# A chained kernel of four layers: in the last one, a block's first products issued ahead of the preceding block's second products

## The chip, the cores and the metric

The program runs on one core of one Trainium2 chip, in one launch. The core has TensorE (PE in the profile, its weight loads shown apart as PEld), VectorE (DVE), ScalarE (ACT), GpSimd (POOL) and SyncE (SP), which only issues transfers here. Each engine works through its own queue of instructions in order; semaphores join them. The metric is the device time of the whole program in microseconds, as the median of the runs.

## The reference, cut to what matters

Four layers follow one another on x of shape (8, 64, 64, 64): a selective scan, a channel and spatial attention, a small network that is trained for two steps on its own input (layer 2), and a spatial attention (layer 3). The change lies where layer 2's trained network is applied and layer 3 begins:

```python
def _modifier(params, x):
    w1, gn_w, gn_b, w2 = params
    h = jnp.einsum('bchw,oc->bohw', x, w1)        # first products
    ...
    h = hg.reshape(b, o, hh, ww) * gn_w[None, :, None, None] + gn_b[None, :, None, None]
    h = _gelu(h)
    return jnp.einsum('bohw,co->bchw', h, w2)     # second products
...
modification = _modifier(params_f, x)
...
return x + residual_scale * gate * modification   # end of layer 2

# layer 3
xb = jnp.einsum('oc,ncl->nol', wb, xf) + bb[None, :, None]
xc = jnp.einsum('oc,ncl->nol', wc, xf) + bc[None, :, None]
xd = jnp.einsum('oc,ncl->nol', wd, xf) + bd[None, :, None]
attention = jnp.einsum('nci,ncj->nij', xc, xb)
att = jax.nn.softmax(attention, axis=-1)
x_o = jnp.einsum('ncj,nij->nci', xd, att).reshape(n, c, h, w)
return alpha[0] * x_o + x
```

## The kernel before, in words

The eight images are worked on in four pairs: the 64 channels of two images fill the 128 partitions, and the 64 x 64 = 4096 positions lie along the free dimension, in NBK = 8 blocks of BK = 512. Everything is float32.

The function `modifier_and_attention` first trains the network (`moments`, then two rounds of `prepare`, `slope`, `gradients`, `update`). In `slope` (L1767 to L1790) the network is applied as well: there the first products of each block are issued one block ahead of the second products, by the list `late`. Then, for each pair p (L2125), it

- loads x of the pair (L2126, `load_pair` at L1635), into one of two buffers;
- applies the trained network block by block (L2127 to L2132): `mod.hidden` makes the first products of both images (L1751, two products of 64 x 512 into the tile hnps) and their Gelu (L1753, two activations of 128 x 512 into the tile a); `mod.output` makes the second products (L1762, two products into the two halves of the tile yps); one VectorE instruction (L2130) adds the gated result to x in place;
- stores x (L2134) for the attention's general case, and a small matrix for each image (L2136);
- makes keys (kps, L1137) and values (vps, L1148) of the whole pair in `att.project`;
- runs the attention in `att.run`: for each block of 512 queries, the query product (qps, L1170) with its bias (L1172), then for 32 groups of 128 keys the scores (sc, L1179), their exponential (ex, L1184), the running sum (L1191) and the values' product (av, L1198). At the end of a block of queries `divide` (L1207 to L1222) sums, takes the reciprocal (L1213) and scales, and `finish` (L2138) adds x and stores the result.

```python
def hidden(self, p, x):
    ...
    ps = self.two()
    ...
    return a
def output(self, a):
    ps = self.bank("yps")
    ...
    return ps
```

The tiles hnps, yps, kps, vps and sc all come from one PSUM pool with three buffers of two banks each (`p_sc`, tag "sc", L2116, L2119, L2120), handed out in turn in the order of the source. The Gelu's tile a has two buffers (tag "h"), the query tile q two, and the query product and the sums of the division share one PSUM bank (`p_psum`, tag "mm", L2115).

The order of instructions on each engine in this part is set by a scheduler that starts from the order of the source and may move an instruction ahead where its inputs are there. In this kernel it has moved the query products of the first three blocks of queries, L1170, from the attention up into the loop of L2127: PE's order there is first products, a query product (in three of the blocks), second products of the same block, first products of the next.

Of the kernel before, what the change touches and what calls it, by code (L numbers as in the profile page):

```python
# [13 lines left out]
ALU = mybir.AluOpType  # L14
# [8 lines left out]
BK = 512  # L23
NBK = L // BK
# [2063 lines left out]
def modifier_and_attention(cm, x2, w, a, x3, mixes, out):  # L2088


    tc, nc = cm.tc, cm.nc
    with ExitStack() as ctx:
        cm.open(ctx, "m_const")
        keep = ctx.enter_context(tc.tile_pool(name="m_keep", bufs=1))
        with ExitStack() as train:
            work = train.enter_context(tc.tile_pool(name="t_work", bufs=2))
            psum = train.enter_context(tc.tile_pool(name="t_psum", bufs=2, space=PSUM))
            mod = Modifier(cm, keep, x2, w, work, psum)
            tok = train.enter_context(tc.tile_pool(name="t_tok", bufs=1))
            wide = train.enter_context(tc.tile_pool(name="t_wide", bufs=2, space=PSUM))  # L2100
            accs = train.enter_context(tc.tile_pool(name="t_acc", bufs=2, space=PSUM))
            mod.two = lambda: wide.tile([128, 2, BK], F32, name="hnps", tag="dps")
            ys = tok.tile([2 * C, NB // 2, L], F32, name="ys")
            mod.moments(tok.tile([128, NB, TQ, C], F32, name="xT"), ys)
            gs = mod.gates()
            for s in range(STEPS):
                mod.prepare(wide)
                mod.slope(ys)
                mod.gradients(ys, wide, accs)
                mod.update(s == 0)  # L2110
            mod.settle()
            mod.prepare(wide)
        work = ctx.enter_context(tc.tile_pool(name="m_work", bufs=2))
        mod.xp = ctx.enter_context(tc.tile_pool(name="m_x", bufs=2))
        psum = ctx.enter_context(tc.tile_pool(name="p_psum", bufs=1, space=PSUM))  # L2115
        sc = ctx.enter_context(tc.tile_pool(name="p_sc", bufs=3, space=PSUM))  # L2116
        avp = ctx.enter_context(tc.tile_pool(name="p_av", bufs=1, space=PSUM))
        mod.psum, mod.work = psum, work
        mod.bank = lambda name: sc.tile([128, 2, BK], F32, name=name, tag="sc")[:, 0, :]  # L2119
        mod.two = lambda: sc.tile([128, 2, BK], F32, name="hnps", tag="sc")  # L2120
        att = Attention(
            cm, ctx, "pa", C, a["wc"], a["bc"], a["wb"], a["bb"], a["wd"], a["bd"],
            a["alpha"], work, psum, sc, avp,
        )
        for p in range(NB // 2):  # L2125
            x = mod.load_pair(mod.xp.tile([2 * C, L], F32, name="x", tag="x"), p, slice(0, L))  # L2126
            for j in range(NBK):  # L2127
                blk = bass.ts(j, BK)
                y = mod.output(mod.hidden(p, x[:, blk]))
                nc.vector.scalar_tensor_tensor(  # L2130
                    x[:, blk], y, gs[:, p : p + 1], x[:, blk], ALU.mult, ALU.add
                )  # L2132

            nc.sync.dma_start(x3[2 * p : 2 * p + 2].rearrange("b c l -> (b c) l"), x)  # L2134
            for b in (2 * p, 2 * p + 1):
                nc.sync.dma_start(mixes[b], cm.ident[:C, :C])  # L2136

            def finish(i, o, p=p, x=x):  # L2138
                blk = bass.ts(i, BK)
                nc.vector.scalar_tensor_tensor(o, o, att.bv, x[:, blk], ALU.add, ALU.add)  # L2140
                nc.sync.dma_start(
                    out[2 * p : 2 * p + 2].rearrange("b c h w -> (b c) (h w)")[:, blk], o
                )

            k, v = att.project(p, x)
            att.run(p, x, k, v, finish)
        bad, src = att.out_of_range(), att.src
    with tc.If(bad > 0):
        general_attention(cm, src, x3, mixes, out.rearrange("b c h w -> b c (h w)"))


@with_exitstack
def conv_seq_kernel(ctx: ExitStack, tc: tile.TileContext, t: dict, out: bass.AP):
    def layer(i):
        p = f"L{i}_conv_"
        return {n[len(p) :]: v for n, v in t.items() if n.startswith(p)}

    dr = ctx.enter_context(tc.tile_pool(name="stream", bufs=1, space=DRAM))
    xh = dr.tile([NB, C, L], F32, name="xh")
    x1 = dr.tile([NB, C, L], F32, name="x1")  # L2160
    x2 = dr.tile([NB, C, L], F32, name="x2")
    x3 = dr.tile([NB, C, L], F32, name="x3")
    mix1 = dr.tile([NB, C, C], F32, name="mix1")
    mix3 = dr.tile([NB, C, C], F32, name="mix3")
    cm = Common(ctx, tc)
    scan_layer(cm, t["x"], layer(0), xh)
    gate_and_attention(cm, xh, layer(0), layer(1), x1, mix1, x2)
    modifier_and_attention(cm, x2, layer(2), layer(3), x3, mix3, out)
# [21 lines left out]
```

## Time and profile before

| | us |
|---|---|
| median of 3 runs | 12229.28 |
| lowest and highest | 12226.62, 12230.54 |
| the profiled execution: its own time | 12228.28 |
| the profiled execution: span of its instructions | 12226.5 |
| PE busy in the span | 11196.6 |
| DVE busy | 10380.4 |
| ACT busy | 7575.7 |
| first products of pair 0 begin | 10102.05 |
| keys begin, pairs 0, 1, 2, 3 | 10134.79, 10661.47, 11189.76, 11716.43 |
| first products begin, pairs 1, 2, 3 | 10631.21, 11157.88, 11686.17 |

The rows with a start are positions in the span, counted from its first instruction. A row of the timeline gives the start of a run of like instructions, how long the run took, the engine, the line of the kernel, the operation and its tiles (written tile first), and in brackets how long the engine had been idle before and which instruction ended that. A row of the stages gives, for a stretch of the span, the busy time of each engine with the number of instructions, then the clock that TensorE was granted (1.00 is full) and the transfers. A matmul's duration in a row overlaps with the next one's, so a distance is read from start to start. A float32 product of one block is two instructions in the profile.

### The profile page before, as it was taken

The numbers are of one execution on the slowest core, as the hardware profiler recorded it, in microseconds if no ns is written. First come the engines' busy times: TensorE is split into PE (matmuls) and PEld (weight loads), VectorE is DVE, ScalarE is ACT, GpSimd is POOL, SyncE is SP. The second block draws the span as 40 slices with busy tenths as digits, with TensorE's granted clock in tenths as the row PEclk, the third lists the DMA queues.
The fourth block names the chain that finished last, engine by engine and source line by source line (L and its number), as shares of the span: only waits on it lengthen the run. The fifth ranks groups of instructions, "written<-read, shape, count | busy, mean of one in ns | idle before, by whom it ended". The sixth has DMA issues, their size and how long they took to land. (4 is left out here: it accounts for less than half of the span.)

```text
span 12226.5 us, 120204 instructions
## 1 busy us (share of the span) xinstructions
PE 11196.6 (92%) x39087; PEld 4103.2 (34%) x39087; DVE 10380.4 (85%) x7400; ACT 7575.7 (62%) x10304; POOL 7247.3 (59%) x3326
## 2 busy tenths in 40 slices
PE   7899999999999999999998799999987779999999
PEld 2233333333333333333322233232335463333333
DVE  4999999999999999999999776868778676676767
ACT  4666667766667676676675554645547574555554
POOL 4999999999999999999999500000007480000000
PEclk8999999999999999999999899999998779999999
DMA  3666666666666666666666400000011100000000
GB/s 112 205 210 217 210 211 214 212 212 210 213 212 207 210 216 209 212 213 211 205 203 211 135 20 25 6 25 8 17 49 34 41 20 24 19 4 19 5 11 6
DMA packets 522899, 1528.62 MB, mean 125 GB/s; under 512 B 125312, under 2 KB 142352, under 8 KB 519696
## 3 DMA queue, kind: packets, MB, share of 16 engines
q1 hardware_dynamic: 522256, 1520.80, 37.9%
q8 instruction: 312, 5.11, 0.2%
q14 instruction: 331, 2.71, 0.1%
HBM read 1439.63 MB, written 72.09 MB: 124 GB/s over the span
## 5 line engine op out<-in xcount | busy, mean ns | idle before, releaser
L816 POOL TENSOR_TENSOR ct<-ct,h 128x1024 f32<-128x1024 f32 x2048 | 4789.4, 2362 | 296.8 <-DVE h L811 133.1
L882 PE MATMUL yps<-ct,lno_cen 128*128 128x512 f32 x8192 | 4119.9, 633 | 58.6 <-ACT yps L869 57.2
L811 DVE TENSOR_TENSOR_SCAN h<-a,state,z 128x1024 f32<-128x1024 f32 x1536 | 3570.4, 2341 | 82.5 <-ACT z L777 39.7
L762 ACT ACTIVATE a<-dt,amat 128x1024 f32<-128x1024 f32 x2048 | 2347.1, 1147 | 1134.8 <-DVE h L811 1128.1
L1191 DVE TENSOR_TENSOR sum<-sum,ex 128x1024 f32<-128x1024 f32 x1920 | 2347.5, 1223 | 618.5 <-ACT ex L1184 483.1
L1184 ACT ACTIVATE ex<-sc 128x1024 f32<-128x1024 f32 x2048 | 1968.0, 1024 | 1359.6 <-PE sc L1179 1359.2
L882 PEld LDWEIGHTS yps<-ct,lno_cen 128*128 128x128 f32 x8192 | 1476.4, 195 | 2078.9 <-issue 1818.0
L807 DVE TENSOR_TENSOR z<-z,e 128x1024 f32<-128x1024 f32 x1536 | 1859.8, 1211 | 128.0 <-PE z L780 75.5
L1198 PE MATMUL av<-ex,v 128*64 128x512 f32 x8192 | 1950.0, 604 | 0.0
L1179 PE MATMUL sc<-q,k 16*128 16x512 f32 (+1 forms) x8192 | 1562.1, 623 | 4.2 <-ACT q L1172 3.1
L780 PE MATMUL z<-bs,pick 48*128 48x512 bf16 x3072 | 941.9, 387 | 388.4 <-DVE h L811 339.5
L811 DVE TENSOR_TENSOR_SCAN h<-a,z 128x1024 f32<-128x1024 f32 x512 | 1161.3, 2281 | 75.0 <-ACT z L777 59.8
L770 POOL TENSOR_TENSOR bt<-bt,e 128x1024 f32<-128x1024 f32 x512 | 1209.8, 2363 | 5.4 <-DMA bt<-bc 5.4
L1505 POOL TENSOR_TENSOR gt<-gt,pad 128x1024 f32<-128x1024 f32 x16 | 34.9, 2179 | 1575.0 <-ACT gt L1504 1575.0
L1198 PEld LDWEIGHTS av<-ex,v 128*64 128x64 f32 x8192 | 512.2, 136 | 1332.7 <-issue 1278.9
L1179 PEld LDWEIGHTS sc<-q,k 16*128 16x128 f32 (+1 forms) x8192 | 528.2, 184 | 1016.4 <-issue 977.4
L777 ACT COPY z<-bt 128x1024 f32<-128x1024 f32 x512 | 519.9, 1015 | 406.0 <-DVE h L811 309.2
L780 PEld LDWEIGHTS <-pick 48*128 48x128 bf16 x3072 | 175.9, 95 | 1514.5 <-DVE h L811 931.4
L534 PE MATMUL vps<-pad,convd 128*128 128x512 f32 x1152 | 573.8, 599 | 0.1
L1878 DVE RECIPROCAL r<-e 128x512 f32<-128x512 f32 x128 | 420.6, 3322 | 0.0
L1881 POOL TENSOR_TENSOR r<-r,half 128x512 f32<-128x512 f32 x128 | 162.7, 1271 | 361.9 <-issue 186.0
L798 ACT COPY state<-h 128x1 f32<-128x1 f32 x2048 | 362.9, 177 | 0.0
(417 smaller groups left out, 9594.8 us busy)
## 6 DMA issues: line engine op xcount, KB each, us to landing
ct<-bc SPq DMA_DIRECT2D x2048, 512.0 KB
bt<-bc SPq DMA_DIRECT2D x512, 512.0 KB
x<-x SPq DMA_DIRECT2D x12, 2048.0 KB
bc<-e SPq DMA_DIRECT2D x128, 128.0 KB
x<-x SPq DMA_DIRECT2D x32, 512.0 KB
part<-x SPq DMA_DIRECT2D x128, 128.0 KB
bsd<-bp SPq DMA_DIRECT2D x192, 64.0 KB
bs<-bsd SPq DMA_DIRECT2D x128, 96.0 KB
```

What stands on the lines that cost most here:

```text
L534: nc.tensor.matmul(held[0].rearrange("p (r c) -> p r c", c=S), convd[:, t, :], pad[:, j * rows + dy : (j + 1) * rows + dy, dx : dx + S], s ...
L762: ctl["exp", n] = nc.scalar.activation(ctl["a", n], ctl["dt"], AF.Exp, scale=amat[:, ctl["k"], n : n + 1])
L770: nc.gpsimd.tensor_tensor(bt, bt, ctl["dus"], ALU.mult)
L780: nc.tensor.matmul(z[:, bass.ts(i, BK)], pick[:, n : n + 1].to_broadcast([3 * N, DI]), ctl["bs"][:, bass.ts(i, BK)], start=True, stop=True,)
L807: first = nc.vector.tensor_tensor(z, z, ctl["dus"], ALU.mult)
L811: nc.vector.tensor_tensor_scan(h[:, flip], a[:, flip], z[:, flip], 0.0 if state is None else state[:, n : n + 1], ALU.mult, ALU.add,)
L816: freed[at] = nc.gpsimd.tensor_tensor(ct, ct, h, ALU.mult)
L882: nc.tensor.matmul(ctl["ps"][:, bass.ts(i, BK)], lno_cen, ct[:, bass.ts(i, BK)], start=False, stop=(n == N - 1 and not ctl["turns"]),)
L1179: nc.tensor.matmul(sc[:, e, :], k[r : r + d, bass.ts(j, 128)], qs[i][r : r + d, :], start=True, stop=True,)
L1184: nc.scalar.activation(ex, sc, AF.Exp)
L1191: nc.vector.tensor_tensor(sums[i], sums[i], ex, ALU.add)
L1198: nc.tensor.matmul(avs[i][r, :], v[:, j, r], ex[:, e, :], start=(j == 0), stop=(j == TQ - 1))
```

## The change

In the loop over the blocks of a pair, the Gelu tiles go into a small table, the loop runs one turn longer, and each turn first issues the first products and Gelu of block j, and then the second products and the update of block j - 1. No computation is added or removed.

```diff
         for p in range(NB // 2):
             x = mod.load_pair(mod.xp.tile([2 * C, L], F32, name="x", tag="x"), p, slice(0, L))
-            for j in range(NBK):
-                blk = bass.ts(j, BK)
-                y = mod.output(mod.hidden(p, x[:, blk]))
-                nc.vector.scalar_tensor_tensor(
-                    x[:, blk], y, gs[:, p : p + 1], x[:, blk], ALU.mult, ALU.add
-                )
+            acts = {}
+            for j in range(NBK + 1):
+                if j < NBK:
+                    acts[j] = mod.hidden(p, x[:, bass.ts(j, BK)])
+                if j:
+                    blk = bass.ts(j - 1, BK)
+                    nc.vector.scalar_tensor_tensor(
+                        x[:, blk], mod.output(acts.pop(j - 1)), gs[:, p : p + 1], x[:, blk],
+                        ALU.mult, ALU.add,
+                    )
```

In the program that comes of it, PE's order in this part is: first products of blocks 0 and 1, then second products and first products in turn, the second products of blocks 6 and 7 one after the other, the keys, the values, and then the query product of the first block of queries. All eight query products of a pair stand behind the values: none is moved into the loop. ScalarE's order follows PE's, and the load of the exponential's table stands behind the first query's bias. The orders of VectorE, GpSimd and SyncE are the same as before.

## The prediction

> **What bounds the kernel now.** I read the chain of waits first, because the change can pay only where it runs.
>
> ```profile
> PE 19%; issue 3%; POOL 1%; DVE 1%; ACT 1%; DMA 0%; SPq 0%; ACTq 0%; DVEq 0%; POOLq 0%
> PE sc L1179 8%; PE av L1198 8%; PE htps L1847 1%; PE acc L1927 1%; PE yps L1762 1%; PE hnps L1751 0%; POOL t L1882 0%; POOL run L1916 0%; POOL t L1883 0%; POOL r L1881 0%; DMA x<-x 0%; ACT L1866 0%; ACT t L1866 0%; PE qps L1170 0%; PE vps L1148 0%
> ```
>
> The followed chain covers the last quarter of the span, and in the last layer it is TensorE (PE). Next the busy time by stage, for the modifier stage of pair 1 and for its attention stage (the columns are the stretch, its length, then PE, PEld, DVE, ACT and POOL busy, PEclk, DMA share, GB/s):
>
> ```profile
> 10630.00:10662.00 32.00, 25.60 (x78) 6.61 (x74) 11.51 (x15) 13.25 (x20) 0.00 (x0) 1.00 0.21 74
> 10700.00:11150.00 450.00, 450.00 (x1950) 150.31 (x1950) 321.74 (x281) 235.93 (x252) 0.00 (x0) 1.00 0.01 5
> ```
>
> In attention PE is never idle, so every microsecond put on or taken off PE there counts in full. In the modifier stage no engine is full: it is a relay. The timeline of pair 1 shows it (start, length, engine, line, operands; in brackets the idle time before and who ended it):
>
> ```profile
> 10631.21 1.13 PE L1751 MATMUL hnps<-x,hwp 64*128 64x512 f32 x4
> ...
> 10632.39 1.26 ACT L1753 ACTIVATE a<-hnps,off 128x512 f32<-128x512 f32 x2
> 10633.13 1.65 PE L1762 MATMUL yps<-a,w2T 128*64 128x512 f32 x4 [0.79 <-ACT a L1753]
> 10634.71 1.13 PE L1751 MATMUL hnps<-x,hwp 64*128 64x512 f32 x4
> ...
> 10637.26 0.74 DVE L2130 SCALAR_TENSOR_TENSOR x<-yps,gp,x 128x512 f32<-128x512 f32 x1
> 10638.06 1.13 PE L1170 MATMUL qps<-x,pa_wq 128*128 128x512 f32 x2 [2.22 <-DVE x L2130]
> ...
> 10650.79 1.13 PE L1751 MATMUL hnps<-x,hwp 64*128 64x512 f32 x4
> ...
> 10652.03 1.26 ACT L1753 ACTIVATE a<-hnps,off 128x512 f32<-128x512 f32 x2 [2.29 <-PE hnps L1751]
> 10652.77 1.65 PE L1762 MATMUL yps<-a,w2T 128*64 128x512 f32 x4 [0.85 <-ACT a L1753]
> 10654.35 1.13 PE L1751 MATMUL hnps<-x,hwp 64*128 64x512 f32 x4
> ```
>
> Call a block's first products h (L1751), its Gelu g (L1753), its second products y (L1762), its update u (L2130). From h to h one block takes 10654.35 - 10650.79 = 3.56 us: h, then PE waits for g, then y. Two things are lost per block: the 0.85 us wait, and y itself, which starts on the first half of g and stretches to 1.58 us (10654.35 - 10652.77) because the second half comes 0.6 us later. Three blocks of a pair also hold one query product (qps, L1170) between h and y; they take 3.56 us too, so those three ride free.
>
> **The change, step by step.** No instruction is added or removed except waits; h and g of block j+1 move ahead of y of block j. h and g issue no DMA, and nothing moves on SP or POOL; DVE's order stays.
>
> *The steady block.* The trace has the same two products in the new order already: the slope pass (L1787), which also issues h one block ahead.
>
> ```profile
> 9162.63 1.13 PE L1751 MATMUL hnps<-x,hwp 64*128 64x512 f32 x4
> ...
> 9163.69 1.08 PE L1762 MATMUL yps<-a,w2T 128*64 128x512 f32 x4
> ...
> 9164.70 1.13 PE L1751 MATMUL hnps<-x,hwp 64*128 64x512 f32 x4
> ...
> 9165.76 2.57 PE L1762 MATMUL yps<-a,w2T 128*64 128x512 f32 x8
> ```
>
> Start to start: h 1.06, y 1.01, so a block is 2.07 us with nothing between. The last row is a run of two y with no h between, 2.50 up to where the next could start: the second one again meets a Gelu half finished. Will g keep up here? It starts 1.24 us after its h (10652.03 - 10650.79) and ends at 2.50; the new order starts y 1.06 + 1.01 + 1.06 = 3.13 after that h. Spare 0.63.
>
> *New wait.* h, y and later kps share three PSUM buffers (tag "sc"). Given out in the order h0 h1 y0 h2 y1 h3 y2 ..., h(j+1) gets the buffer of y(j-2) and so waits for u(j-2). In the steady part u ends 0.1 + 0.75 us after its y, and h(j+1) comes 2.07 us after it: no stall. Behind h on PE stand all later products, so at a pair's start the wait does bite: u0 stands behind the previous pair's last division on DVE and ends at 10638.0 (row 10637.26 + 0.74). h3 cannot start before 10638.06, exactly where the query product waits today. PE has then done h0 h1 y0 h2 y1, against h0 y0 h1 before.
>
> *Pairs 1 and 3.* From 10638.06 there remain h3 to h7, y2 to y5, and the two last y: 5 x 1.06 + 4 x 1.01 + 2.50 = 11.84, so the keys (kps) start at 10649.90 instead of 10661.47: 11.57 saved; pair 3 has the same spacing. *Pair 2* spends 1.62 us more today (31.88 from first h to kps against 30.26), at a granted clock of 0.50 from 11165.9 to 11169.3. I weigh that below and take 11.57 again.
>
> *Pair 0* starts cold: PE waited for x until 10102.05, and the granted clock is 0.50 until 10111.0. y0 can start where it does now, 10106.53, and ends at 10109.0 as now, or near 10108.3 if the clock comes up one window (3.41 us) earlier because PE is denser. After it come 6 h, 5 y and the two last y, 13.91 us; h2 alone takes about 1 us more in the cold case. So kps starts near 10122.2 or 10123.9; today 10134.79. Saved 10.9 to 12.6; I take 11.7.
>
> Sum of the stages: 3 x 11.57 + 11.7 = 46.4 us.
>
> *What is given back.* The cover of the three query products goes with the relay. In the changed program they stand after the values product (vps) and inside attention. What one costs there is in the trace, where the other five of a pair already stand:
>
> ```profile
> 10799.49 2.79 PE L1198 MATMUL av<-ex,v 128*64 128x512 f32 x12
> 10802.21 1.12 PE L1170 MATMUL qps<-x,pa_wq 128*128 128x512 f32 x2
> 10803.27 2.85 PE L1179 MATMUL sc<-q,k 64*128 64x512 f32 x12
> ```
>
> 1.06 us each on a full PE; 3 x 1.06 = 3.18 a pair. And the first scores now wait for the first query, while today they follow vps at once:
>
> ```profile
> 10668.44 7.31 PE L1148 MATMUL vps<-pa_wv,x 128*128 128x128 f32 x64
> ...
> 10675.67 5.42 PE L1179 MATMUL sc<-q,k 64*128 64x512 f32 x24
> ```
>
> qps to its bias activation takes 1.16 us (10638.06 to 10639.22), the activation 0.69, the hand-over 0.05: scores start 1.90 after vps, 0.84 beyond the product itself. No row shows this wait in place. Lower bound 0.84; upper 2.1, if the table load (1.28 us), which ACT now runs after the query bias, came on top. I take 0.84, because the load ends about when the first scores do (1.18 us after their start) and three score buffers cover the rest. Given back: 4 x (3.18 + 0.84) = 16.1.
>
> **Sum:** 46.4 - 16.1 = 30.3 us. Against the profiled execution's 12228.28 this gives 12198.0; the median of the runs is 1.0 above that execution, so 12199. I write **12198.5**.
>
> [...] In the last layer the idle time before the y rows ended so:
>
> ```profile
>   ACT a L1753: 69.7, 78
> ```
>
> It is the Gelu, not a buffer set free by DVE; with the buffer count above I go with the row.
> [...]
>
> **Rivals.** (a) *g always half late:* y stays at 1.58, as each waiting y of this stage shows; the slope row speaks against it. Some 21 middle y lose 0.57: 12 us, time 12210, inside no change. (b) *Too few buffers, or the order without effect:* the relay stays, only the queries are lost: 12244. Speaks for it: the shared three buffers; against: the count of buffers, and PE's order in the changed program, where h(j+1) stands ahead of y(j). (c) *Better:* clock up early, no cold window, packed products: 12192. (d) *Slower:* PE drops to half clock in the modifier stages, triggered by the boundary gap that cools one pair in three today. A window costs 1.62; from 30.3 / 1.62 = 19 windows on, some five a pair, the gain is gone, and with the whole dense stage cold (8 x 2.07 = 16.6 more a pair) the time is 12264. Against it: the window after a busy one is granted in full everywhere here.
>
> **Chances.** Forecast 0.74, (c) 0.04, (a) 0.14, (b) 0.05, (d) 0.03. What a measurement can tell from no change is 0.2%, 24.5 us: faster means below 12204.8. So faster 0.78, same 0.19, slower 0.03. Range: from (c) with the runs' spread of 2 us to (a), 12190 to 12210; (b) and (d) are left out.
>
> **What would show it.** h and y alternating every 2.07 us with y rows of 1.08; kps some 11.6 us earlier after a pair's first h (18.7 instead of 30.3); one h waiting for u near 6.9 us after it; 1.9 us between vps and the scores; one query row before the first scores, one after the first values and one in the next block of queries. A y of 1.5, h waiting on u in every block, or score groups longer than 5.50 us would prove me wrong.

## The result, and the profile after

| | before | after |
|---|---|---|
| median of 9 runs each, us | 12228.19 | 12194.06 |
| lowest and highest, us | 12219.06, 12237.64 | 12184.21, 12202.81 |
| profiled execution, its own time, us | 12228.28 | 12199.93 |
| span of the profiled execution, us | 12226.5 | 12198.2 |
| first h of pair 0 to the last instruction ("last part"), us | 2124.4 | 2090.7 |

The ratio of the times is 0.9972, 95% interval 0.9963 to 0.9981: 34 us less. The spread of the runs, some 20 us, can be laid to the part of the span ahead of pair 0, which the change does not touch: the first h of pair 0 stood anywhere from 10088 to 10114 us in the profiles of this study, with the same code ahead of it. So all that follows is read in the last part, and there mostly in distances within a pair, which in pairs 1 to 3 of these two kernels repeat to 0.01 us where the granted clock was 1.00 (30.26 and 30.26, 18.69, 18.68 and 18.68 us from first h to first keys).

As before, h, g, y, u are a block's first products, Gelu, second products and update. The chain of waits of the changed kernel:

```profile
PE 20%; POOL 2%; DVE 2%; issue 1%; ACT 1%; DMA 1%; SPq 0%; DVEq 0%; POOLq 0%; ACTq 0%
PE sc L1179 8%; PE av L1198 8%; PE htps L1847 1%; PE hnps L1751 1%; PE yps L1762 1%; PE acc L1927 1%; POOL t L1882 1%; DMA x<-x 1%; POOL run L1916 1%; POOL r L1881 1%; POOL t L1883 0%; PE qps L1170 0%; DVE r L1878 0%; PE vps L1148 0%; PE kps L1137 0%
```

PE still carries it. The same two stages of pair 1, in the columns used before (stretch, length, busy PE, PEld, DVE, ACT, POOL, granted clock, transfers):

```profile
10627.00:10647.00 20.00, 18.78 (x70) 4.76 (x67) 11.44 (x15) 11.88 (x18) 0.00 (x0) 1.00 0.34 119
10700.00:11140.00 440.00, 440.00 (x1905) 146.69 (x1903) 314.72 (x275) 230.38 (x246) 0.00 (x0) 1.00 0.01 5
```

The modifier stage has become a stage of 20 us instead of 32 and is nearly full on PE; attention is as full as it was. The timeline of PE in pair 1:

```profile
10627.76 1.99 PE L1751 MATMUL hnps<-x,hwp 64*128 64x512 f32 x8
10629.68 1.65 PE L1762 MATMUL yps<-a,w2T 128*64 128x512 f32 x4
10631.26 1.13 PE L1751 MATMUL hnps<-x,hwp 64*128 64x512 f32 x4
10632.32 1.08 PE L1762 MATMUL yps<-a,w2T 128*64 128x512 f32 x4
10634.61 1.13 PE L1751 MATMUL hnps<-x,hwp 64*128 64x512 f32 x4 [1.22 <-DVE x L2133]
10635.67 1.08 PE L1762 MATMUL yps<-a,w2T 128*64 128x512 f32 x4
10636.68 1.13 PE L1751 MATMUL hnps<-x,hwp 64*128 64x512 f32 x4
...
10643.95 2.57 PE L1762 MATMUL yps<-a,w2T 128*64 128x512 f32 x8
10646.45 7.13 PE L1137 MATMUL kps<-x,pa_wk 128*128 128x512 f32 x16
10653.42 7.31 PE L1148 MATMUL vps<-pa_wv,x 128*128 128x128 f32 x64
10660.56 1.02 PE L1170 MATMUL qps<-x,pa_wq 128*128 128x512 f32 x2
10662.36 5.42 PE L1179 MATMUL sc<-q,k 64*128 64x512 f32 x24 [0.78 <-ACT q L1172]
```

From 10634.61 to 10636.68 is one block: 2.07 us, no idle time in brackets, y back to 1.08. Three things stand out of the row: one h that waits 1.22 us for the first update, the run of the two last y, and the first scores, which wait 0.78 us for the query's bias. In the last layer, idle time ahead of y that the Gelu ended fell from 69.7 us to

```profile
  ACT a L1753: 23.6, 34
```

The whole difference, in distances of PE's timeline (pair 0 of the kernel before from the row of its first h, 10102.08; the 10102.05 given above is the weight load just ahead of it):

| us | pair 0 | pair 1 | pair 2 | pair 3 | sum of the changes |
|---|---|---|---|---|---|
| first h to first keys, before | 32.72 | 30.26 | 31.88 | 30.26 | |
| after | 20.07 | 18.69 | 18.68 | 18.68 | -49.0 |
| values to first scores, before | 7.23 | 7.23 | 7.24 | 7.24 | |
| after | 8.94 | 8.94 | 8.95 | 8.94 | +6.8 |
| first scores to the next pair's first h (or the end), before | 482.21 | 482.21 | 482.20 | 495.86 | |
| after | 484.32 | 484.32 | 484.32 | 498.01 | +8.5 |

-49.0 + 6.8 + 8.5 = -33.7 us, the difference of the two last parts, and about that of the medians (-34.1).

### The profile page after: what moved, and what is told of

It is laid out like the page before. It is cut to its first block, busy times and chain, and to the rows that moved or that the text cites. A ratio compares the mean times of both kernels' runs of the same rounds, so it can differ in the third digit from the quotient of the medians.

```text
span 12198.2 us, 120204 instructions
## 1 busy us (share of the span) xinstructions
PE 11171.0 (92%) x39087; PEld 4099.5 (34%) x39087; DVE 10381.2 (85%) x7400; ACT 7575.8 (62%) x10304; POOL 7249.5 (59%) x3326
```

## The experiments

An experiment for which no ratio is given was run once, and is read in its profile alone.

### Only the query products behind the values

```diff
+            mm = nc.tensor.matmul(ps, self.wq, x[:, bass.ts(i, BK)], start=True, stop=True)
+            cm.tc.add_manual_dep(mm.ins, self.last_v.ins.name, ...)   # order only: after the last values product
```

on the kernel before; the loop over the blocks stays as it was.

> The old loop (first products, Gelu, second products, update of one block, then the next), with the one difference that all eight query products of a pair stand behind the values, as in the changed kernel. Theory 1 (the gain is the relay taken apart; moving the three query products is a cost beside it): blocks stay at 3.56 us, first h to first keys of pairs 1 to 3 is 28 to 29 us (the wait of a query on the first update is gone, some 1.9 us), values to scores takes 1.7 to 1.8 us more, and each attention stage about 3.8 us more; last part (first h of pair 0 to the last instruction) 2128 to 2134 us against 2124.4 of the kernel before and 2090.7 of the changed one. Theory 2 (the query products between h and y were what made the block long): blocks fall towards 2.1 us, h to keys towards 19, last part below 2100.

Measured: last part 2132.4 us, first h to first keys 28.62, 28.34 and 28.34 us in pairs 1 to 3 (32.72 in pair 0), values to scores 8.94, first scores to next h 484.32. The whole: 12236.91 against 12230.58, ratio 1.0010 (1.0001 to 1.0019). PE in its steady part:

```profile
10636.74 1.13 PE L1756 MATMUL hnps<-x,hwp 64*128 64x512 f32 x4
10638.72 1.65 PE L1767 MATMUL yps<-a,w2T 128*64 128x512 f32 x4 [0.85 <-ACT a L1758]
10640.30 1.13 PE L1756 MATMUL hnps<-x,hwp 64*128 64x512 f32 x4
```

3.56 us a block, with no query between. So the query products did not make the block long: they filled its gap. Moving them out costs 8.0 us of the last part by itself, and the step from here to the changed kernel (2132.4 to 2090.7) is 41.7 us: that is what issuing h ahead is worth.

### The old loop, but second products in a bank of their own

```diff
-                y = mod.output(mod.hidden(p, x[:, blk]))
+                y = mod.output(
+                    mod.hidden(p, x[:, blk]), avp.tile([128, BK], F32, name="yav", tag="av")
+                )
```

on the kernel before: y leaves the three shared buffers for the PSUM bank of the attention's values, which is idle in this stage.

> The old loop in the source, but the second products go into the attention's own PSUM bank, idle at that time, and no longer share the three buffers with the first products. Theory 1 (the source's order makes the relay; buffers have no part in it): blocks of 3.56 us as before, first h to first scores of pairs 1 to 3 about 44.5 us, last part about 2124. Theory 3 (the shared three buffers, handed out in the source's order, are what kept the first products of the next block behind: with a bank of its own for y, the scheduler issues them ahead by itself): blocks of 2.07 us, first h to first scores 34 to 35 us as in the changed kernel (34.6), last part 2088 to 2094.

Measured: ratio to the kernel before 0.9972 (0.9962 to 0.9982), last part 2097.3 us, first h to first scores 35.60 us in pairs 1 and 3 and 37.22 in pair 2. PE in pair 1:

```profile
10625.12 2.84 PE L1751 MATMUL hnps<-x,hwp 64*128 64x512 f32 x10
10627.89 1.08 PE L1762 MATMUL yav<-a,w2T 128*64 128x512 f32 x4
10628.89 1.13 PE L1751 MATMUL hnps<-x,hwp 64*128 64x512 f32 x4
10632.06 1.08 PE L1762 MATMUL yav<-a,w2T 128*64 128x512 f32 x4 [2.04 <-DVE x L2132]
10633.07 1.13 PE L1751 MATMUL hnps<-x,hwp 64*128 64x512 f32 x4
10634.13 1.08 PE L1762 MATMUL yav<-a,w2T 128*64 128x512 f32 x4
```

The source still says h, y, h, y, and yet two and a half h stand ahead of the first y (h is four instructions) and a block takes 2.07 us. So the source's order alone does not make the relay; it takes the buffers shared with y as well.

It was not their number. Handed out in turn, h(j+1) gets the buffer that held y(j-1), and in the kernel before that one was free in time:

```profile
10650.90 0.75 DVE L2130 SCALAR_TENSOR_TENSOR x<-yps,gp,x 128x512 f32<-128x512 f32 x1 [2.81 <-PE yps L1762]
```

This update ends at 10651.65, when h(j), begun at 10650.79, has still 0.2 us of its 1.06 to go; and the changed kernel runs its 2.07 us on the same three buffers. What fits both kernels is the order in which they go out: in the source's order the buffer of h(j+1) comes after that of y(j), and the scheduler, which had moved query products ahead on its own, left h behind. The change turns that order; another bank takes y out of it. That this is how the scheduler decided is inferred: the runs do not look into it.

One bank for all y has its price: y1 waits for the first update (2.04 us), and keys get in between the last y. The scores of pairs 1 and 3 come 1.0 us later than in the changed kernel, and the last part is 6.6 us longer, 1.6 us of it by a stretch of half clock in pair 2 (18.89 us from first h to first keys against 17.27; the granted clock was 0.87 from 11150 to 11154 and 0.70 from 11154 to 11158). Both are above what I expected.

### The wait for the first update

```diff
-                        x[:, blk], mod.output(acts.pop(j - 1)), gs[:, p : p + 1], x[:, blk],
+                        x[:, blk], mod.output(acts.pop(j - 1), avp.tile(...) if j == 1 else None), gs[:, p : p + 1], x[:, blk],
```

on the changed kernel: only y of block 0 goes into the other bank.

> The changed kernel, with only the second products of block 0 of each pair in the attention's own idle bank; then no first products wait for the first update, which stands behind the previous pair's last division on VectorE. Theory 1 (that wait is a wait for a buffer): the stall of 1.2 us in pairs 1 to 3 goes, first h to first scores 33.3 to 33.6 us instead of 34.60; pair 0 unchanged within 0.3. Rival (VectorE is behind with its updates): the stall appears at the next product, 34.4 to 34.7.

Measured: first h to first scores 33.58 us in pairs 1 to 3 (34.60), first h to keys 17.67 (18.68). No h in these pairs waits, as pair 1 shows:

```profile
10637.80 2.84 PE L1751 MATMUL hnps<-x,hwp 64*128 64x512 f32 x10
10640.57 1.08 PE L1762 MATMUL yav<-a,w2T 128*64 128x512 f32 x4
10641.57 1.12 PE L1751 MATMUL hnps<-x,hwp 64*128 64x512 f32 x2
10642.63 1.08 PE L1762 MATMUL yps<-a,w2T 128*64 128x512 f32 x4
10643.64 1.13 PE L1751 MATMUL hnps<-x,hwp 64*128 64x512 f32 x4
...
10643.84 0.75 DVE L2133 SCALAR_TENSOR_TENSOR x<-yav,gp,x 128x512 f32<-128x512 f32 x1
```

h3 starts at 10643.64, before the first update has even begun. So the 1.22 us were a wait for a buffer, and VectorE, whose updates come later, does not hold PE up. The saving is not the wait alone, since PE's order moved as well: as in the experiment before, half of h2 now stands ahead of y0 and its other half behind.

The expectation for pair 0 missed: 23.83 us to the keys instead of 20.07. There the granted clock was 0.50 until some 13 us after the first h, against some 5 in the changed kernel's profile, though PE had no idle time:

```profile
10115.67 3.72 PE L1751 MATMUL hnps<-x,hwp 64*128 64x512 f32 x6
10119.33 1.97 PE L1762 MATMUL yav<-a,w2T 128*64 128x512 f32 x4
10121.23 2.07 PE L1751 MATMUL hnps<-x,hwp 64*128 64x512 f32 x2
10123.24 1.98 PE L1762 MATMUL yps<-a,w2T 128*64 128x512 f32 x4
...
10120.00:10124.00 4.00, 4.00 (x8) 0.79 (x6) 0.75 (x1) 0.60 (x2) 0.00 (x0) 0.50 0.00 0
```

The half of h2 at 10121.23 takes 2.01 us to the next start by itself. Why the clock stayed down this run cannot say; the last experiments bear on it.

### Two blocks ahead

```diff
-            for j in range(NBK + 1):
+            for j in range(NBK + 2):
...
-                if j:
+                if j >= 2:
```

with y and u of block j - 2, and three Gelu tiles instead of two.

> The changed kernel with first products two blocks ahead instead of one, and three Gelu tiles instead of two. Theory 1 (PE is full in the steady part, only ends and boundaries are left): blocks stay at 2.07 us, no gap between the last second products, the wait for the first update shrinks from 1.2 us to 0.2 or less; first h to first scores 33.0 to 33.3 us in pairs 1 to 3 instead of 34.60. Rival (three first products in three buffers starve the second products): blocks of 2.3 us or more, 35 us or more.

Measured: first h to first scores 32.76 us in pairs 1 to 3, to the keys 16.84; last part 2083.8.

```profile
10632.94 1.13 PE L1753 MATMUL hnps<-x,hwp 64*128 64x512 f32 x4 [0.93 <-DVE x L2135]
10634.00 1.08 PE L1764 MATMUL yps<-a,w2T 128*64 128x512 f32 x4
10635.00 1.13 PE L1753 MATMUL hnps<-x,hwp 64*128 64x512 f32 x4
...
10640.20 2.79 PE L1764 MATMUL yps<-a,w2T 128*64 128x512 f32 x12
```

The block stays at 2.06 us: one block ahead already filled PE, as expected. What goes are the ends: the three last y run in 2.79 without a stop. The wait for the first update shrank only to 0.93 us, not 0.2, because y0 no longer waits for half of its Gelu (1.01 us to the next start instead of 1.58) and PE is there sooner; the total gain was somewhat larger than expected.

### The first query ahead of the last second products

```diff
+                    if j == NBK + 1 - 1:
+                        q0 = att.query(x, 0)
...
-            att.run(p, x, k, v, finish)
+            att.run(p, x, k, v, finish, q0)
```

on the changed kernel, with PE's order in the loop fixed as written.

> The changed kernel with the first query product of a pair issued between the second products of blocks 6 and 7 instead of behind the values. Theory 1: there it falls into the 0.5 us in which the last second products wait for their Gelu, and the wait of the first scores for the query (1.8 us from query to scores) is gone: first h to first keys 19.2 to 19.4 us in pairs 1 to 3 (18.69 in the changed kernel), values to scores 7.23 (8.94), first h to first scores 33.4 to 33.6 (34.60). If the wait for the query was not what stood behind the values, values to scores stays near 8.9.

Measured in pairs 1 to 3: 19.25 us from first h to keys, 7.24 from values to scores, 33.46 from first h to first scores; last part 2086.1. The query and its bias were what stood between values and scores, and the query costs only 0.57 us in the gap of the last y.

### The halves alternate

```diff
-    h0 h1 | y0 y1        (both halves of h, then both halves of y)
+    h0 y0 | h1 y1        (one half of h, one half of y)
```

as the order on PE within a turn of the changed loop; the queries stand behind the values. The same products are made.

> The changed kernel, but each of the two first products of a block is followed by one of the two second products of the preceding block, so that no two half-width products of the same kind stand side by side on PE; queries behind the values. Theory 1 (the 2.07 us of a block need the two half-array products side by side; each takes about as long alone as a full-width product, 0.87 us by the keys): blocks of 3.3 to 3.7 us, first h to first keys of pairs 1 to 3 of 28 to 31 us, as slow as the relay. Rival (a half-width product takes half the time wherever it stands): blocks of 2.1 us, 18 to 20 us.

Measured: first h to first keys 32.0 us in pairs 1 to 3, 58.75 in pair 0; last part 2170.1. PE in pair 1:

```profile
10661.69 1.12 PE L2143 MATMUL hnps<-x,hwp 64*128 64x512 f32 x2
10662.74 1.07 PE L2148 MATMUL yps<-a,w2T 128*64 128x512 f32 x2
10663.74 1.12 PE L2143 MATMUL hnps<-x,hwp 64*128 64x512 f32 x2
```

One half (x2) now takes 1.05 or 1.00 us, as much as both halves side by side (x4) in the changed kernel; a block is 4.11 us, not the 3.3 to 3.7 I expected. I had reckoned with the 0.87 us of a full product among the keys (6.97 us for eight); a half that follows one of the other kind takes 0.13 to 0.18 us more. The direction holds: PE is never idle in these rows and yet slower than the relay. The 2.07 us stand on the two halves side by side.

### Both gains together

Two blocks ahead with the early query, and then also y of block 0 in the other bank.

> First products two blocks ahead, three Gelu tiles, and the first query product before the last second products. Theory 1: the gains of both add up less the gap that is filled only once: first h to first keys 17.8 to 18.0 us in pairs 1 to 3, values to scores 7.23, first h to first scores 32.0 to 32.2; last part some 8 to 10 us under the changed kernel's 2090.7.

> As the kernel with two blocks ahead and the early query product, and also the second products of block 0 in the attention's idle bank, so that no first products wait for the first update. Theory 1: the stall of 0.9 us goes too, first h to first scores 31.1 to 31.3 us in pairs 1 to 3; last part 2078 to 2082 us; the whole some 0.35% under the kernel before. Rival (VectorE behind with its updates): the stall stays, 32.0 or more.

Measured: 32.25 us from first h to first scores in pairs 1 to 3, just above what I expected, and a last part of 2081.2 for the first; 31.26 and 2078.8 for the second. Against the kernel before the ratios are 0.9967 (0.9955 to 0.9979) and 0.9960 (0.9947 to 0.9974). The second has no stop left between its first h and its scores in pair 1:

```profile
10606.58 2.85 PE L1763 MATMUL hnps<-x,hwp 64*128 64x512 f32 x12
10609.35 1.08 PE L1774 MATMUL yav<-a,w2T 128*64 128x512 f32 x4
10610.36 1.13 PE L1763 MATMUL hnps<-x,hwp 64*128 64x512 f32 x4
...
10621.56 1.13 PE L1162 MATMUL qps<-x,pa_wq 128*128 128x512 f32 x2
10622.62 1.08 PE L1774 MATMUL yps<-a,w2T 128*64 128x512 f32 x4
```

It is 11.9 us shorter in its last part than the changed kernel. The intervals of the two ratios (0.9960 here, 0.9972 for the changed kernel) overlap, so the gain over the changed kernel is shown by the trace and not by the whole time.

### The clock of pair 0

Pair 0 took 58.75 us in the alternating kernel, far more than the others. So, on the changed kernel, the halves alternate in pair 0 alone; and in a second one only in its later blocks:

```diff
-                for e in range(2): h half e, then y half e
+                turns = [h0, h1, y0, y1] up to y of block 3, then [h0, y0, h1, y1]
```

The two diffs of this kind are orders of products, not text of the code.

> The changed kernel with the halves of first and second products alternating in pair 0 alone, which starts after a wait at half clock; pairs 1 to 3 as in the changed kernel, queries behind the values. Theory 4 (PE that works on half of its array all the time does not bring the clock up, though it is never idle): pair 0 stays at a granted clock of 0.50 up to its keys, blocks of 3.9 us, wait: 8 half-width turns at half clock make 7.9 to 8.0 us a block, first h to first keys 57 to 60 us; pairs 1 to 3 18.7. Rival (the clock comes up after a few us of steady work, and the one look before was chance): first h to first keys 35 to 45 us.

> As before, but in pair 0 the halves stand side by side up to the second products of block 3 and alternate from then on. Theory 4 with a memory (half-width work cannot raise the clock but does not lower it once it is up, as pairs 1 to 3 of the alternating kernel show): the clock comes up in the first 5 to 14 us and stays at 1.00, alternating blocks take 4.1 us, first h to first keys 27 to 33 us. Rival (half-width work lets the clock drop in this place): a granted clock of 0.50 again before the keys, blocks of 8 us, 38 us or more.

Measured in pair 0: 58.74 us from first h to first keys for the first, 26.54 for the second, a little under the expected 27; and 18.68 or 18.69 in all other pairs of both. The stages of pair 0, first of the kernel that alternates from the start:

```profile
10089.00:10094.00 5.00, 4.20 (x8) 1.66 (x9) 0.69 (x3) 2.26 (x3) 0.00 (x0) 0.50 0.77 328
10094.00:10146.00 52.00, 52.00 (x55) 10.61 (x56) 4.51 (x6) 9.13 (x15) 0.00 (x0) 0.50 0.00 0
```

and of the one that alternates late:

```profile
10089.00:10094.00 5.00, 4.39 (x10) 2.05 (x11) 0.69 (x3) 2.45 (x4) 0.00 (x0) 0.50 0.76 324
10094.00:10101.00 7.00, 7.00 (x26) 1.75 (x26) 2.25 (x3) 3.78 (x7) 0.00 (x0) 0.92 0.00 0
10101.00:10114.00 13.00, 13.00 (x28) 2.95 (x26) 2.25 (x3) 4.45 (x8) 0.00 (x0) 1.00 0.00 0
```

In the first, PE is busy for 52.00 of 52 us at a granted clock of 0.50, and the clock comes up 1.7 us into the keys behind it. In the second, the clock is up after 6 us of halves side by side, and 13 us of alternation keep it at 1.00. In the kernel with y0 in the other bank half of h2 stands alone twice, and the clock was 0.50 until 12.6 us after the first h; in the kernel with both gains no half stands alone, y0 has the same bank, and the clock was up after 5.7 us. So with h issued ahead the clock came later where halves stood alone. Why, these runs do not show: the order on PE changes at once how much of the array is in use (64*128 or 128*64 of 128*128 in the rows) and how often h and y take turns.

## Why the prediction was right, step by step

- **The bound and the block.** Relay before, 2.07 us a block after, as the slope pass had it: exact. The 41.7 us between the first experiment and the changed kernel show that issuing h ahead is the cause, and not the moved queries.
- **The new wait.** h3 started 10634.61 - 10627.76 = 6.85 us after the first h, as foretold (6.9). The gap in front of it was 1.22 us. It is the wait for the buffer of y0: with another bank it is gone.
- **Pairs 1 and 3.** 11.57 and 11.58 us saved; forecast 11.57.
- **Pair 2.** Saved 13.20, forecast 11.57. That pair 2 would save no more than pairs 1 and 3 is a term of the sum that no run shows: the stretch at 0.50 that cost the kernel before 1.62 us there did not come in the changed kernel, whose clock was 1.00 from 11143 to 11165. Over all profiles, a stretch of half clock followed in 2 of 6 boundaries of pairs 1 to 3 with a gap over 2 us (pair 2 of the kernel before, 2.22; pair 2 of the old loop with the other bank, 2.03), and in none of 30 whose longest gap was 1.22 or less. So the change, which shortens the gap from 2.22 to 1.22 us, should have been credited with the 1.62 us. The length of the gap does not settle it, though: after the same gap of 2.22 us pairs 1 and 3 of the kernel before stayed at 1.00. And in an earlier attention of the kernel before, whose scores use 16 rows (sc, 16*128), the half clock followed a stretch with no gap over 0.78 us:

```profile
8110.84:8114.25 3.41, 2.61 (x14) 0.69 (x12) 3.30 (x2) 1.52 (x2) 0.00 (x0) 1.00 0.00 0
8114.25:8117.66 3.41, 3.17 (x8) 1.04 (x10) 3.31 (x3) 3.05 (x4) 0.00 (x0) 0.50 0.02 5
```

- **Pair 0.** Saved 12.65, just above my 10.9 to 12.6. The clock came up 5.3 us after the first h instead of 9.0 before, the better of the two cases that I had allowed for. In the six profiles with h issued ahead and no half alone at the start of pair 0 it took some 4.5 to 6 us, by the clock of the stages or the length of the rows, so that was the usual case, and my middle value of 11.7 was too careful. With half of h2 alone it took 9.1 us (the old loop with the other bank) and 12.6 us (y0 in the other bank); in the last only 8.9 us were saved. That the order on PE may bear on the clock in this way stood nowhere in my forecast.
- **What is given back.** 3 products at 1.06 and the wait: 4.02 a pair forecast, 3.8 measured. The wait with its query took 1.71 instead of 1.90 us: about half of the difference is that the query starts earlier behind the values' last, short products (7.14 us against 7.23), the other half that the scores follow 1.80 us after the query's start. The table load on ScalarE did not add to it, since the rest of attention grew by 2.11 us, just the two other queries: its upper bound was not needed. The early query, which takes the wait away, shows that this term was real.
- **The sum.** 49.0 - 15.3 = 33.7 against 46.4 - 16.1 = 30.3. The forecast of 12198.5 was 4.4 us above the median; 1.6 of it is pair 2's clock, 1.0 pair 0, 0.8 the give-back, and the last 1.0 lies within the spread of the stages ahead.
- **The rivals.** (a) is out: y rows are 1.08 in the steady part. (c) came nearer than the forecast: 12192 against 12194.06, since two of its terms came true, the early clock of pair 0 and no cold window; I had given it 0.04. (d) is out: the clock is 1.00 in every stage of pairs 1 to 3. But the argument against it, that the window after a busy one is granted in full, does not hold everywhere: where the halves alternate in pair 0, 52.00 busy us of 52 were granted 0.50, and from 8018.68 to 8028.92 of the kernel before 10.24 of 10.24. (b) did not come true, but the argument with which I put it aside was only half right. I read from the waits that the Gelu and not a buffer held y up. That names who released y; it does not say why PE had nothing else to do. The old loop with the other bank shows that the buffers had a part in that: given one more bank, the old source runs at 2.07 us a block instead of 3.56. Three buffers were enough in number, as I had counted; what mattered is whom they are shared with and in which order they go out.

## What to carry to other kernels

When a chain of small products waits on another engine in every block, ask first what keeps the next block's products behind: where a scheduler orders the work, a ring of buffers that two kinds of product share, handed out in the source's order, can hold them to that order, and either another order in the source or a bank apart undoes it. Count what fills the gap today: three query products were free in the relay and cost 1.06 us each in the full stage. And judge the steady part from a place in the same trace where the new order already runs; here it gave 2.07 us to the hundredth.

## What the hardware showed that I had not expected

- Two products that use half of PE's rows (h, 64*128) or half of its columns (y, 128*64) took 1.06 or 1.01 us together in the changed kernel, where they are neighbours, and 1.05 or 1.00 us each in the kernel whose row halves and column halves alternate. There a block took 4.11 us instead of 2.07.
- In the alternating order at the start of pair 0 PE did not come up from 0.50: it was busy for 52.00 of 52 us at that clock where pair 0 alone alternates, and for 44.00 of 44 us where all pairs do, and a half took 2.01 or 1.89 us there instead of 1.05 or 1.00. Once the clock was up, the same work did not bring it down: 13.00 busy us of 13 in pair 0 of the kernel that alternates late were granted 1.00, and so were the 30 us from 10653 in pair 1 of the kernel that alternates throughout, whose pairs 2 and 3 took the same 32.0 us.
